# Keys instead of queries masked in a 16-head causal attention, two heads' 64 keys per weight tile, attended values packed for one projection pass (fp32, attention and top-2 mixture of experts on one core)

## The chip, the cores and the metric

One Trainium2 chip, one of its cores. TensorE (PE) does matmuls, PEld is its weight load, VectorE (DVE), ScalarE (ACT) and GpSimd (POOL) do elementwise work, SyncE (SP) issues DMAs; ACT and POOL issue some too. The metric is the device time of one launch in microseconds; lower is better. A profile is one execution, recorded by the hardware.

## What is computed

Sixteen sequences of 256 tokens with 128 features, all in fp32, the weights included:

```python
qkv = (x @ w_qkv).reshape(B, S, 3, 16, 8)
Q, K = apply_rope(Q), apply_rope(K)
attn = softmax(where(causal, Q K^T * 8**-0.5, -1e9))
x1 = layernorm(x + (attn @ V) @ w_proj + b_proj)
logits = x1 @ W_router + b_router
top_vals, top_idx = top_k(logits, 2)            # of 8 experts
w = softmax over the two chosen logits
y = sum over the chosen e of w_e * (relu(x1 @ W1[e] + b1[e]) @ W2[e] + b2[e])
out = layernorm(x1 + y)                         # W1: 128 x 512, W2: 512 x 128
```

## The kernel before

**How the order is set.** The kernel does not issue its instructions where it defines them. `Plan.op` (L441) only records an operation: an engine, a cost (used by the planner that made the order, offline), a function that issues it, what it reads and writes, and for some an alternative on another engine. `emit` (L482) then issues all of them in the order of a literal list, `ORDER` (L339); a second list, `OTHER` (L328), names those that take their alternative engine. Each engine runs its own instructions strictly in that order and waits for others by semaphores. Buffers come from pools that all stages share: k1, k2, k4, k8 in SBUF (1, 2, 4, 8 KB a partition) and, in PSUM, `ps_sc` (one tile of four banks), `ps_o` (one) and `ps_m` (three).

**Attention of one sequence** (`attention(b)`, L830). Transpose x (L837), project q and k (L858), rope on DVE (L866 to L871). The 16 heads of 8 features lie in four row groups of 32 partitions, four heads in each. To use a whole row group for one head, `mask_q` makes four copies of q, each with the rows of one head kept (ACT L881 or DVE L891). A score matmul (L953) has 128 keys of one row group as weights (32 x 128) and two or four masked query copies as 512 moving columns; there are three rounds of four matmuls. The first two have keys 0 to 127 against all queries of two of the four heads, the third keys 128 to 255 against the upper 128 queries of all four. Each round fills the one `sc` tile, ACT takes its exp (L986, 128 x 2048) into SBUF, and POOL sets the entries above the diagonal to zero (`affine_select`, L963, over the first 128 queries of each head).

`weigh` (L1003) multiplies with the values: weights are 32 columns that hold one head's eight values and a column of ones, the ones giving the softmax's denominators; 16 matmuls of 256 columns and 16 of 128. The result has two halves `t`. It is copied out (`o_out`, ACT L1020 or DVE L1024), a DMA gathers the 16 denominators' rows (`load_den`), DVE takes reciprocals (L1039), a DMA puts them back (`load_back`), `stream_shuffle` spreads them over the partitions (L1052, 512 elements), a product divides (L1063, 512), and `project_o` multiplies by w_proj in two passes, one for each half (L1074, four matmuls); the bias is a row of that weight. Then residual (L1086), layernorm statistics (L802, L803) and scaling (L1104). The values come from `project_v` (L904, two matmuls that also give x's part of the router's logits) and are put in place by `place_v` (ACT L913 and L917, or DVE L921 and L925).

**Routing.** The sequences are in four chunks of 4, 4, 2 and 6 (`CHUNKS`). For each, `route` (L1188) takes the two largest logits (DVE L1206 to L1228), counts tokens for each expert (PE L1235), works out addresses (L1240 to L1262; an iota on POOL at L1267), and scatters each token's row to its expert's place in a DRAM heap by indirect DMAs on POOL (L1278): 64 in the program.

**Experts.** 48 calls of `block` (L1490) do 128 or 256 rows each: load rows and weights (SP), transpose (L1537, out by L1564 or L1570), first layer (L1576), relu (ACT L1589 or DVE L1598), second layer (L1606), bias (DVE L1615), the routing weight (ACT L1624 or DVE L1633), and an indirect DMA of each 128 rows to the token's place in DRAM (`send`, POOL L1642, 69 in all). They come in two phases; the last holds the chunk of six sequences. `combine` (L1708) reads the rows back, adds them to x1 (PE L1767 for the last phase, DVE L1777 and L1778 for the other), normalizes and stores. While the last rows are fetched, dummy matmuls run (`keep_warm`, L1875 and L1879, `WARM` = 12). `check` (L1886) looks for overflow; a general path that it would start is not run here.

Of the kernel before, what the change touches and what calls it, by code (L numbers as in the profile page):

```python
# [21 lines left out]
P = 128  # L22
HEADS = 16
HD = 8
# [281 lines left out]
RECIPROCAL = [i // (2 * HD) * (2 * HD) + HD + 1 for i in range(32)]  # L306

WARM = 12
# [20 lines left out]
0 1 4 5 15 16 20 21 27 29 31 32 35 36 37 41 49 51 52 54 68 82 83 84 85 87 102 113 119 122 138  # L329
139 152 154 155 171 185 189 191 208 218 260 261 262 264 281 288 295 297 314 330 331 358 395 428  # L330
451 462 472 474 489 498 503 524 540 559 572 591 594 602 604 610 758 774 797 806 826 838 845 854
857 870 889 890 893 918 925 934 941 953 954 979 994 997 1010 1033 1036 1044 1046 1057 1058 1061
1080 1084 1106 1109 1110 1123 1132 1148 1149 1152 1162 1163 1171 1179 1187 1193 1201 1202 1210
1218 1226 1234 1241 1254 1259 1267 1272 1280 1282 1295 1306 1308 1311 1319 1332 1337 1347 1350
1360 1363 1371 1397 1402 1410 1415 1423 1425 1438 1441 1449 1462 1467 1475 1488 1493 1513 1518
1525 1532 1534 1540
# [3 lines left out]
7 2 0 3 1 6 5 44 27 45 4 28 46 77 9 11 47 53 78 36 48 79 51 52 29 49 12 50 114 30 115 54 61 31  # L340
80 116 62 32 147 148 55 63 117 149 118 81 39 119 83 56 86 58 87 57 85 121 59 122 254 217 82 150
33 218 10 64 8 21 60 151 88 84 35 89 65 184 91 16 185 605 120 19 123 92 66 15 17 255 67 94 90 93
95 68 155 97 154 96 219 20 124 22 131 98 220 606 37 69 18 186 13 221 132 125 187 153 99 70 100
126 101 102 193 127 128 133 152 129 156 188 613 223 134 14 23 130 158 159 42 71 192 157 24 135
190 103 104 136 189 105 161 160 357 25 72 26 358 137 162 194 138 73 163 287 164 165 139 106 288
167 168 224 166 195 191 196 256 222 74 257 198 169 199 75 41 258 107 262 170 140 201 225 200 260
202 289 197 359 231 259 171 108 76 172 232 141 203 109 204 173 290 226 110 291 228 227 263 293
233 142 205 111 143 229 112 174 206 113 360 234 207 235 34 294 175 144 176 230 261 264 268 177
269 208 361 145 324 292 296 178 271 427 325 236 146 394 270 179 180 395 607 272 181 237 182 295
183 238 265 364 626 239 266 326 627 240 327 267 328 209 428 301 628 273 241 365 362 274 275 302  # L350
276 303 298 629 331 242 634 299 210 243 497 630 277 278 304 305 211 363 297 330 632 396 300 244
633 307 306 631 332 397 374 641 640 498 375 279 333 636 308 280 368 398 281 212 369 245 499 366
282 309 310 371 399 402 311 246 367 642 334 372 611 247 213 370 637 604 635 214 283 215 248 38
338 284 376 400 312 313 329 339 567 377 373 285 340 335 314 378 500 639 568 315 336 379 638 380
501 316 341 40 337 286 643 216 381 317 318 612 249 504 506 344 342 250 319 251 401 405 320 406
429 343 648 646 408 619 321 253 322 323 345 645 252 647 534 652 346 653 505 382 654 409 535 507
651 411 412 347 656 43 403 650 503 383 407 404 348 655 414 502 430 384 410 511 657 644 349 658
431 512 415 433 350 536 351 413 508 660 649 432 416 659 385 386 509 667 434 435 352 353 417 387
418 514 515 354 663 537 388 444 665 538 355 542 569 389 445 356 570 390 441 391 510 392 517 513
516 464 393 465 678 518 679 543 680 519 541 540 446 442 436 666 520 539 662 438 437 668 661 664  # L360
681 439 571 682 419 684 521 443 574 618 685 420 696 440 544 573 551 421 552 447 669 683 697 686
522 545 698 422 546 572 672 676 575 699 448 449 548 466 671 675 690 549 609 615 581 688 523 621
800 687 467 468 622 582 450 451 553 700 471 578 423 579 547 701 755 850 472 554 469 610 832 550
883 771 702 473 576 866 867 674 584 689 424 425 931 1014 880 608 990 470 914 977 426 555 524 673
556 784 963 585 670 452 691 453 964 557 804 772 525 475 577 454 476 882 852 677 474 694 770 693
526 896 786 692 695 614 848 849 527 580 455 881 583 946 801 456 478 865 703 1026 528 457 785 620
586 477 479 558 481 559 625 458 753 1002 756 459 529 587 560 835 884 961 588 482 853 851 589 590
854 787 855 561 483 885 591 754 856 886 805 858 806 820 788 1029 484 592 916 480 485 486 487 802
932 460 857 752 488 789 888 461 790 704 859 489 1003 890 593 860 803 490 757 887 758 976 868 889
562 594 759 761 792 794 791 1015 808 900 491 595 596 462 928 793 810 769 492 891 1027 861 493  # L370
863 962 463 494 833 563 892 495 893 597 760 960 564 598 836 929 762 599 894 773 768 1012 1013
915 496 565 864 763 566 795 816 530 531 600 764 601 774 602 862 765 532 767 533 1016 807 817 603
1000 987 796 766 999 775 776 809 811 777 1017 705 778 706 707 812 709 779 1018 710 895 974 965
708 713 780 1019 813 815 781 966 1040 869 711 1041 1025 712 1020 1001 623 837 1038 783 838 870
967 1004 1005 739 748 814 968 819 723 871 989 743 991 840 992 714 898 873 986 821 842 1021 872
749 975 948 750 822 1022 1116 720 834 1030 1031 874 944 719 718 839 725 1006 978 841 843 724
1007 1433 945 1238 721 969 716 973 844 979 993 994 912 1510 715 747 717 1237 970 1028 722 1023
1024 933 934 824 1008 826 875 1404 913 782 726 980 1009 734 897 1250 1508 727 981 818 1090 1329
936 728 732 938 823 735 917 899 971 876 731 1051 982 1460 988 825 983 935 901 736 984 745 1507
937 730 737 1103 918 995 1509 1277 1407 919 1485 996 738 949 902 1354 733 1355 921 1032 1142  # L380
1317 950 930 729 1033 920 1064 922 939 923 845 940 903 997 924 624 1356 740 1482 972 904 925 744
1484 827 1251 1302 1408 1042 927 926 797 1313 947 847 1129 1555 906 746 1326 741 742 905 952 954
951 828 953 1034 907 1065 1066 1091 1380 1035 1434 1239 955 1420 1067 1077 1469 1092 1010 1069
985 1235 1052 1472 846 1011 956 1036 998 908 1117 1068 877 1071 1093 1417 1094 1070 1443 1078
957 959 1053 617 1054 1072 1073 1096 1055 1057 1095 1118 1104 1391 1056 1119 1143 1097 1079 879
1120 1037 1058 1039 1074 941 1395 1080 1382 1330 1121 1122 829 798 1098 878 1263 1432 1130 1274
1105 1303 1106 1099 1082 1076 1100 1144 1059 1381 1123 1084 1043 1081 1145 909 1419 1131 1044
751 1060 1369 958 1262 1107 1083 1045 831 1132 1109 1046 1147 1108 799 1124 1252 1343 1261 1102
1275 1287 1110 1101 942 1146 1248 1125 911 1075 1406 1126 1394 1353 1149 830 1047 910 1288 1133
1048 1265 1379 1279 1421 1049 1148 1134 1304 1378 1280 1352 1291 1135 943 1278 1357 1249 1061  # L390
1111 1358 1292 1314 1293 1150 1367 1136 1266 1393 1267 1085 1112 1050 1368 1458 1137 1301 1151
1359 1062 1063 1365 1113 1152 1290 1305 1128 1115 1138 1473 1127 1139 1289 1268 1264 1456 1114
1236 1339 1086 1430 1294 1360 1306 1300 1269 1140 1295 1276 1431 1253 1254 1281 1328 1327 1087
1383 1361 1270 1362 1282 1384 1271 1141 1445 1255 1283 1240 1272 1154 1256 1241 1307 1284 1318
1319 1257 1435 1285 1242 1470 1258 1436 1089 1259 1316 1153 1437 1308 1315 1243 1331 1438 1385
1244 1088 1418 1363 1219 1187 1486 1245 1447 1211 1260 1386 1246 1320 1332 1309 1195 1474 1321
1220 1247 1475 1296 1221 1422 1273 1310 1471 1366 1163 1387 1203 1364 1297 1188 1388 1476 1322
1423 1196 1222 1439 1298 1179 1311 1477 1392 1189 1340 1323 1171 1197 1424 1389 1342 1483 1324
1312 1396 1198 1397 1478 1370 1444 1390 1440 1299 1223 1398 1204 1371 1341 1479 1425 1399 1344
1205 1345 1333 1164 1190 1155 1426 1487 1427 1441 1334 1372 1212 1335 1325 1428 1286 1191 1480  # L400
1400 1488 1373 1336 1172 1401 1224 1192 1405 1409 1489 1337 1459 1410 1374 1165 1457 1402 1225
1448 1429 1490 1449 1213 1411 1193 1481 1375 1491 1492 1346 1412 1493 1206 1226 1199 1446 1347
1450 1376 1214 1451 1442 1413 1338 1461 1215 1414 1348 1415 1200 1227 1207 1349 1403 1173 1350
# [85 lines left out]
def main_path(  # L489
# [244 lines left out]
    def turn_w():  # L734
        for t in range(2):
            nc.tensor.transpose(ps_w.get()[:, t, :], wproj_sb[:, t, 0:D], ident)
# [1271 lines left out]
```

## Time and profile before

| | |
|---|---|
| Time, three runs | median 429.5 us (427.94 to 432.92) |
| Profiled execution | 430.44 us; its span, first to last instruction, 428.4 |
| Exp L986 | 48 of 1.88 us |
| Causal mask L963 on POOL | 48, 67.3 us |
| Scores L953 / weigh L1003 on PE | 60.6 / 56.7 us |
| Scatter L1278 / send L1642 on POOL | 64 of 0.99 / 69 of 0.99 us |
| Indirect DMA's spacing in a row | 1.28 us (0.97 and 0.30 of issue) |
| Last second layer ends, span ends | 405.5, 428.4 us |

Busy time is the time in which an engine works. In a group's row stand the line, the engine, the tiles and shapes, the number of records, then busy time and the mean of one, then idle time before them and what ended it. One fp32 matmul leaves two records (so "x8" of L953 is a round of four). `<-remote` is a release that the profile can't assign, `issue` is time in which the engine waited for nothing that it shows.

### The profile page before, as it was taken

How to read it: one execution, taken by the hardware profiler on the slowest of the kernel's cores; microseconds unless marked ns; L12 is line 12 of the kernel's file. 1: busy time of each engine (PE TensorE's matmuls, PEld its weight loads, DVE VectorE, ACT ScalarE, POOL GpSimd, SP SyncE). 2: the span in 40 equal slices, each digit the busy share in tenths (PEclk: the TensorE clock that was granted, in tenths of full speed). 3: DMA queues.
4: the chain of work that ended last, by engine and by line, in shares of the span. 5: the costliest groups of instructions: out<-in, count | busy, mean ns of one | idle time of the engine just before them, and what ended most of it. 6: DMA issues, size and time to landing. Idle time of an engine off the chain costs nothing.

```text
span 428.4 us, 8846 instructions
## 1 busy us (share of the span) xinstructions
PE 339.9 (79%) x2811; PEld 242.0 (56%) x2811; DVE 244.3 (57%) x843; ACT 202.6 (47%) x400; POOL 211.3 (49%) x241
## 2 busy tenths in 40 slices
PE   5899999988879786779997539189984896968981
PEld 3444555445434332455896438079873796958870
DVE  2945688995889772644778302015442533575783
ACT  1667778757756653534455211043240322445742
POOL 2346343357786667753025736603467164344432
PEclk9999999998998978969999859669997996997996
DMA  6210020024011015214273445722444443550173
GB/s 190 80 52 8 4 55 3 3 56 68 22 47 29 15 56 159 65 51 115 60 203 114 137 132 141 215 84 87 131 116 123 118 135 100 178 163 29 36 224 107
DMA packets 48436, 39.75 MB, mean 93 GB/s; under 512 B 13807, under 2 KB 38004, under 8 KB 48386
## 3 DMA queue, kind: packets, MB, share of 16 engines
q1 hardware_dynamic: 32658, 26.35, 22.3%
q0 software_dynamic: 4256, 8.47, 5.8%
q10 hardware_dynamic: 11472, 4.31, 4.1%
q8 instruction: 25, 0.41, 0.4%
q14 instruction: 25, 0.20, 0.2%
HBM read 26.90 MB, written 12.01 MB: 91 GB/s over the span
## 4 chain that ended last, share of the span: by engine, by line
PE 46%; issue 13%; DVE 12%; ACT 12%; POOL 7%; another core or an unknown queue 6%; DMA 2%; ACTq 0%; POOLq 0%; DVEq 0%
PE m L1576 13%; PE m L1606 13%; ACT pr L986 9%; PE sc L953 8%; PE ps_o L1003 5%; POOL heap L1278 4%; PE m L1074 3%; POOL pr L963 2%; PE m L858 1%; DVE st L802 1%; PE ps_o L1537 1%; DMA wqk_sb<-in_L_attn_w_qkv_dram 1%; ACT hT L1589 1%; DVE y L1615 1%
## 5 line engine op out<-in xcount | busy, mean ns | idle before, releaser
L1642 POOL DMA_INDIRECT back<-y,rows_in x69 | 68.2, 989 | 104.2 <-ACT y L1624 55.2
L986 ACT ACTIVATE pr<-sc 128x2048 f32<-128x2048 f32 x48 | 90.1, 1878 | 56.3 <-PE sc L953 35.1
L1576 PE MATMUL m<-rT,w 128*128 128x128 f32 (+1 forms) x384 | 77.8, 349 | 33.2 <-DVE y L1615 18.9
L963 POOL TENSOR_SCALAR_AFFINE_SELECT pr<-pr 128x1024 f32<-128x1024 f32 (+1 forms) x48 | 67.3, 1412 | 73.6 <-ACT pr L986 73.5
L1576 PEld LDWEIGHTS m<-rT,w 128*128 128x128 f32 x384 | 61.5, 210 | 41.5 <-DVE y L1615 20.1
L1589 ACT ACTIVATE hT<-m,b_sb 128x128 f32<-128x128 f32 (+1 forms) x124 | 42.2, 417 | 83.9 <-PE m L1576 32.9
L1606 PE MATMUL m<-w_sb,hT 128*128 (+1 forms) x552 | 73.5, 288 | 4.5 <-ACT hT L1589 3.0
L1278 POOL DMA_INDIRECT heap<-x_sb,dest x64 | 63.5, 992 | 22.7 <-issue 20.3
L1606 PEld LDWEIGHTS m<-w_sb,hT 128*128 128x128 f32 x552 | 69.9, 203 | 7.8 <-ACT hT L1589 4.4
L953 PE MATMUL sc<-qTm,qk 32*128 32x512 f32 x384 | 60.6, 673 | 15.1 <-ACT pr L986 12.4
L1003 PE MATMUL ps_o<-pr,va 128*32 128x128 f32 (+1 forms) x1024 | 56.7, 345 | 6.1 <-issue 5.3
L1615 DVE TENSOR_TENSOR y<-m,b_sb 128x128 f32<-128x128 f32 (+1 forms) x48 | 16.7, 348 | 74.9 <-remote 31.5
L1003 PEld LDWEIGHTS ps_o<-pr,va 128*32 128x32 f32 x1024 | 29.6, 113 | 36.9 <-issue 21.8
L953 PEld LDWEIGHTS sc<-qTm,qk 32*128 32x128 f32 x384 | 16.9, 193 | 31.3 <-ACT pr L986 22.7
L1598 DVE TENSOR_SCALAR hT<-m,b_sb 128x128 f32<-128x128 f32 (+1 forms) x68 | 23.3, 399 | 19.7 <-PE m L1576 11.6
L1074 PE MATMUL m<-wproj_sb,o 128*128 128x136 f32 x128 | 20.6, 308 | 4.8 <-issue 3.3
L1074 PEld LDWEIGHTS m<-wproj_sb,o 128*128 128x128 f32 x128 | 18.0, 206 | 11.1 <-issue 5.5
L866 DVE TENSOR_TENSOR part<-m,rope_sb 128x512 f32<-128x512 f32 x16 | 10.9, 680 | 22.5 <-PE m L858 22.4
L858 PE MATMUL m<-xT,wqk_sb 128*128 128x256 f32 x64 | 20.5, 451 | 1.0 <-DMA wqk_sb<-in_L_attn_w_qkv_dram 0.7
L1624 ACT ACTIVATE y<-y,rows_in 128x128 f32<-128x128 f32 x41 | 14.8, 401 | 13.2 <-DVE y L1615 11.5
L881 ACT ACTIVATE qTm<-qk,rows_sb 128x256 f32<-128x256 f32 x40 | 19.5, 506 | 2.1 <-DVE qk L871 2.1
L858 PEld LDWEIGHTS m<-xT,wqk_sb 128*128 128x128 f32 x64 | 12.5, 215 | 11.4 <-issue 5.4
(183 smaller groups left out, 381.5 us busy)
## 6 DMA issues: line engine op xcount, KB each, us to landing
w<-in_L_ffn_W_dram SPq DMA_DIRECT2D x48, 256.0 KB
rows_in<-heap SPq DMA_DIRECT2D x21, 130.0 KB
ys<-back SPq DMA_DIRECT2D x10, 256.0 KB
w_sb<-in_L_ffn_W_dram SPq DMA_DIRECT2D x7, 256.0 KB
rows_in<-heap SPq DMA_DIRECT2D x27, 65.0 KB
ys<-back ACTq DMA_DIRECT2D x6, 256.0 KB
x<-in_L_attn_x_dram ACTq DMA_DIRECT2D x9, 128.0 KB
out_dram<-yout SPq DMA_DIRECT2D x9, 128.0 KB
```

Source lines behind the costliest of these rows:

```text
L858: nc.tensor.matmul(ps_qk.get()[:, s, :], wqk_sb[:, s, :], xT.get(), start=True, stop=True)
L953: nc.tensor.matmul(ps.get()[:, g], qk.get()[rg, 1, ts(kt, P)], qTm.get()[rg, js, kt * P : S], start=True, stop=True,)
L963: nc.gpsimd.affine_select(out=pr.get()[:, :, :, 0:P], in_=pr.get()[:, :, :, 0:P], compare_op=ALU.is_ge, fill=0.0, base=0, pattern=[[0, GRO ...
L986: lambda pr=pr, ps=ps: nc.scalar.activation(pr.get(), ps.get(), AF.Exp),
L1003: nc.tensor.matmul(pso.get()[ts(g, 32), t, kt * P : S], va_t[:, kt, 2 * g + t].rearrange("p u c -> p (u c)")[:, 16 * u : 16 * u + 32], pr. ...
L1074: nc.tensor.matmul(ps_p.get()[:, q, :], o.get()[:, t, ts(q, P)], wproj_sb[:, t, :], start=(t == 0), stop=(t == 1),)
L1278: nc.gpsimd.indirect_dma_start(out=heap[:, :], out_offset=bass.IndirectOffsetOnAxis(ap=dest[:, k, t : t + 1], axis=0), in_=x1_sb[:, t, 0:D ...
L1576: nc.tensor.matmul(ps_h[i].get()[:, c, :], w.get()[:, ts(i * per + c, P)], rT.get()[:, 0 : n * P], start=True, stop=True,)
L1589: nc.scalar.activation(hT.get()[:, at, 0 : n * P], ps_h[i].get()[:, c, :], AF.Relu, bias=bias)
L1598: V.tensor_scalar(hT.get()[:, at, 0 : n * P], ps_h[i].get()[:, c, :], bias, 0.0, ALU.add, ALU.max)
L1606: nc.tensor.matmul(ps_y.get()[:, i, :], hT.get()[:, c, i * P : (i + 1) * P], w2_sb[:, e, c, :].rearrange("p o d -> p (o d)"), start=(c == ...
L1642: put = nc.gpsimd.indirect_dma_start(out=back[:, :], out_offset=bass.IndirectOffsetOnAxis(ap=rows_in.get()[:, i, D : D + 1].bitcast(I32), ...
```

## The change

- **Scores.** The keys are masked instead of the queries. A weight tile holds 64 keys of two heads, one head's 64 columns after the other's (32 x 128), and q itself is the moving side. The tile of 64 keys number c needs only the queries from 64c on. The rounds are: c = 0 (8 matmuls of 256 columns), c = 1 and 3 together (8 of 192, 8 of 64), c = 2 (8 of 128). The exps are of 2048, 2048 and 1024 elements.
- **Causal mask.** Only one 64 x 64 corner of each head is cut: a product with a table of 0 and 1 (`triangle`) over 512, 1024 and 512 elements in place of `affine_select` over 1024, 1024 and 2048. It may run on POOL or DVE; `OTHER` puts 24 of 48 on DVE (15 of 512 and 9 of 1024).
- **Values.** 128 rows hold 64 keys of two heads. `project_v` has eight matmuls with 64 output columns each; `place_v` copies two half-height parts, and the router's part is an operation of its own (`place_r`). Value weights hold both heads in 32 columns, values and ones interleaved; `weigh` has 8 matmuls of 256 columns, then 8 of 192 and 8 of 64, then 8 of 128.
- **Output.** The two halves `t` occupy alternate rows. A new DMA, `pack` (64 KB, one a sequence; 8 on SP's queue, 8 on ACT's), puts the second half's rows between the first half's. Reciprocals go to a tile of their own, shuffle and division take 256 elements instead of 512, and `project_o` is one pass of two matmuls. The bias is added to x beforehand (`x_bias`, 5 on POOL, 11 on DVE).
- **Last blocks.** Of the last phase the last two single blocks (`HOT` = 2) are neither weighed nor sent; POOL sends rows of zeros in their place, early. DVE builds a matrix with the routing weight at each row's token (128 x 1536, compared with token numbers that an iota writes), and PE adds it times the block's result to the sums (`add_here`, 12 times two matmuls of 128 x 128 x 128). `WARM` goes from 12 to 5.
- Pool sizes: k1 19, k2 16, k4 7, k8 5 instead of 18, 18, 5, 6. New literals `ORDER` and `OTHER`. In POOL's new order three masks stand between the scatters of chunks 1 and 2 instead of 15.

```diff
-WARM = 12
+HALF = P // 2
+WARM = 5
+HOT = 2
...
-        qTm = buffer(k4, "qTm", [P, 4, S])
+        kTm = buffer(k4, "kTm", [P, 2, S // HALF, 2, HALF])
...
-                lambda j=j: nc.scalar.activation(
-                    qTm.get()[:, j, :], qk.get()[:, 0], AF.Copy, scale=rows_sb[:, j : j + 1]
-                ),
+            def rows_of_head(j=j):
+                into = kTm.get()[:, j // 2, :, j % 2, :]
+                return into, qk.get()[:, 1].rearrange("p (c k) -> p c k", k=HALF), rows_sb[:, j : j + 1]
+            def mask_k(of=rows_of_head):
+                into, from_, own = of()
+                nc.scalar.activation(into, from_, AF.Copy, scale=own)
...
-            for t in range(NT):
+            for c in range(S // HALF):
+                for u in range(2):
+                    n = VW + E if u == c % 2 else VW
                     nc.tensor.matmul(
-                    ps_v.get()[:, t, :],
-                    xT.get()[:, ts(t, P)],
-                    wvr_sb,
+                        ps_v.get()[u * HALF : (u + 1) * HALF, c // 2, c % 2, 0:n],
+                        xT.get()[:, c * HALF : (c + 1) * HALF],
+                        wv_sb[:, u, 0:n],
...
+        def add_bproj(engine):
+            engine.tensor_tensor(xt.get(), xt.get(), bproj_sb.to_broadcast([P, NT, DR]), ALU.add)
...
+        rounds = [[(0, 0)], [(1, 0), (3, S - HALF)], [(2, 0)]]
+        rounds = [[(t, c, at) for t in range(2) for c, at in r] for r in rounds]
...
-            ps = tile_of(ps_sc, "sc", [P, GROUPS, nj, nq])
-            pr = buffer(k8, "pr", [P, GROUPS, nj, nq])
+            ps = tile_of(ps_sc, "sc", [P, GROUPS, 2, S])
+            pr = buffer(k8 if r < 2 else k4, "pr", [P, GROUPS, 2, nq])
...
-                        ps.get()[:, g],
-                        qk.get()[rg, 1, ts(kt, P)],
-                        qTm.get()[rg, js, kt * P : S],
+                            ps.get()[:, g, t, at : at + S - c * HALF],
+                            kTm.get()[rg, t, c].rearrange("p u k -> p (u k)"),
+                            qk.get()[rg, 0, c * HALF : S],
...
-                nc.gpsimd.affine_select(
-                    out=pr.get()[:, :, :, 0:P],
-                    in_=pr.get()[:, :, :, 0:P],
+                cut = pr.get().rearrange("p g t (b q) -> p (g t) b q", q=HALF)
+                cut = cut[:, :, 0 : 4 : 3] if r == 1 else cut[:, :, 0:1]
+                keep = triangle.rearrange("p (a b q) -> p a b q", a=1, b=1)
+                engine.tensor_tensor(
+                    cut, cut, keep.to_broadcast([P, 2 * GROUPS, 2 if r == 1 else 1, HALF]), ALU.mult
+                )
...
-                            va_t[:, kt, 2 * g + t].rearrange("p u c -> p (u c)")[
-                                :, 16 * u : 16 * u + 32
-                            ],
-                            pr.get()[:, g, 2 * t + u if kt else u, :],
+                            va_t[:, c, 2 * g + t, :],
+                            pr.get()[:, g, t, at : at + S - c * HALF],
...
+            lambda: load(o.get()[1:P:2, 0, :], o.get()[0:P:2, 1, :]),
+            writes=[o],
+            what="pack",
...
-                for t in range(2):
-                    nc.tensor.matmul(
-                        ps_p.get()[:, q, :],
-                        o.get()[:, t, ts(q, P)],
-                        wproj_sb[:, t, :],
+                nc.tensor.matmul(
+                    ps_p.get()[:, q, :], o.get()[:, 0, ts(q, P)], wproj_sb, start=True, stop=True
+                )
...
-                in_=y.get()[:, i, :],
+                in_=nothing if direct else y.get()[:, i, :],
...
+            def place():
+                V.tensor_scalar(
+                    of_row.get(), all_tokens.get(), token.get()[:, 1:2],
+                    rows_in.get()[:, 0, D + 1 : DX], ALU.is_equal, ALU.mult,
+                )
...
+                            put = nc.tensor.matmul(
+                                acc[b].get()[:, i, :], of_row.get()[:, b, i, :], y.get()[:, 0, :],
+                                start=False, stop=False, skip_group_check=True,
+                            )
```

## The prediction, made before the changed kernel was run

> **What bounds the kernel now.** I read the page first (busy shares, chain, groups), then the windows by stage, then the chain of waits inside the attention, then the timeline where the engines go quiet.
>
> ```profile
> PE 339.9 (79%) x2811; PEld 242.0 (56%) x2811; DVE 244.3 (57%) x843; ACT 202.6 (47%) x400; POOL 211.3 (49%) x241
> 6.00:86.00 80.00, 74.05 (x768) 39.48 (x772) 59.62 (x158) 56.01 (x65) 32.64 (x47) 1.00 0.14 39
> 86.00:126.00 40.00, 34.60 (x357) 18.99 (x345) 32.19 (x102) 25.64 (x35) 28.52 (x26) 0.96 0.23 50
> 126.00:154.00 28.00, 23.43 (x215) 11.49 (x213) 23.12 (x72) 16.00 (x24) 19.37 (x18) 0.94 0.09 26
> 154.00:199.40 45.40, 34.16 (x288) 18.25 (x287) 23.46 (x96) 21.93 (x23) 27.03 (x29) 0.81 0.35 98
> 199.40:405.50 206.10, 160.52 (x1150) 144.14 (x1147) 91.37 (x342) 72.34 (x228) 93.55 (x97) 0.88 0.42 120
> 405.50:428.40 22.90, 12.44 (x55) 9.22 (x53) 14.50 (x76) 9.05 (x27) 7.17 (x14) 0.85 0.53 156
> ```
> The rows after the first are stretches: length, then busy time of PE, PEld, DVE, ACT, POOL, then clock and DMA. I cut them at the routing counts of chunks 0, 1 and 2 (PE L1235: 86, 126, 154 us), the first expert block's transpose (199.4) and the last second layer (405.5). Up to 86 us PE is busy for 93% of the time, DVE for 75%. From 86 to 154 DVE is nearest its limit (81%). From 154 on no engine is.
>
> ```profile
> 11.95 1.18 PE sc L953 x8
> 13.12 0.02 issue
> 13.15 1.89 ACT pr L986
> 15.03 0.04 issue
> 15.08 1.19 PE sc L953 x8
> 16.26 0.02 issue
> 16.28 1.89 ACT pr L986
> ```
> The chain (start, length) shows why PE is full and yet waits: one score tile in PSUM, so score (1.18) and exp (1.89) alternate. A round takes 15.08 - 11.95 = 3.13, three a sequence 9.4 us. The other matmuls run under the exps.
>
> ```profile
> 247.43 0.97 POOL L1278 DMA_INDIRECT heap<-x_sb,dest  x1 [0.30 <-issue]
> 248.70 0.97 POOL L1278 DMA_INDIRECT heap<-x_sb,dest  x1 [0.30 <-issue]
> 249.98 0.97 POOL L1278 DMA_INDIRECT heap<-x_sb,dest  x1 [0.30 <-issue]
> 253.05 0.29 DVE L1615 TENSOR_TENSOR y<-m,b_sb 128x128 f32<-128x128 f32 x1 [8.08 <-remote]
> 253.11 0.84 ACT L1589 ACTIVATE hT<-m,b_sb 128x256 f32<-128x256 f32 x2 [10.51 <-remote]
> 253.39 1.22 PE L1576 MATMUL m<-rT,w 128*128 128x256 f32 x2 [7.89 <-DVE y L1615]
> ```
> The last is a stall of everything. POOL issues 12 indirect DMAs in a row (235.9 to 251.0, one per 1.28 us); after about the fifth the other engines start almost nothing until 2 us past the last. The same stands at 157.7-166.5 (7 in a row), 173.1-184.6 (9), 259.2-277.1 (14) and 319.7-332.2 (10). The idle times there add up to about 41 us, some 15 of them in the attention.
>
> **PE.** Scores: before, three rounds of 4 matmuls of 512 columns (L953, 8 records, 1.17). After, 8 x 256, then 8 x 192 + 8 x 64, then 8 x 128. By columns this is 1, 1 and 1/2 of the old round, 2.9 us for 3.5; by weigh's row (L1003: 1.00 for 8 matmuls of 256, 1.01 for 16 of 128) 2.5. Against it: weight loads of 128 columns go from 12 matmuls to 32, 64 records a sequence. L953's 384 loads fill 16.9 us, 0.044 each, because four row groups load together; wholly exposed that is 64 x 0.044 = +2.8. Range 2.5 to 5.8; I take 3.0, near the column count, since loads are already overlapped in that row. Weigh: 3.01 before; after 1.00 + 1.01 + 0.50 = 2.5. Output projection (L1074): 4 matmuls 1.12, after 2, 0.56. Value projection (L904): 2 matmuls 0.73, after 8 short ones with 64 output columns: 0.5 (half the columns in pairs) to 1.06 (L858's row); I take 0.8. Per sequence -0.5 -0.5 -0.56 +0.07 = -1.5, times 16 = -24 us, all in the attention. The new `add_here` is 12 x 2 matmuls of 128 x 128: 0.45 each by half of L1606 (8 records, 0.89), 1.05 by L1767; 7 fewer dummies (L1879, 0.45) give 3.2 back.
>
> The Trainium skill, "TensorE: Matmul & The Clock Gate", section LDWEIGHTS, says that a load's time goes by its columns and not by its rows, so a 32-row load costs what a 128-row one does. That speaks against 64 loads in place of 24. L953's mean load is 193 ns and L1003's, of 32 columns, 113 ns, which agrees. One after another they would be 64 x 0.193 = 12.4 us a sequence and the change far slower; the row's 16.9 us for 384 says they overlap.
>
> **ACT.** Exps: two of 1.88 and one of half the size, 0.94 to 1.0; -0.92 x 16 = -15 us. Six fewer head masks on ACT -3. The value copies become two of 64 partitions (0.37 to 0.74 more each sequence) +6, four more L1020 copies +2, 12 more DMA issues on ACT's queue x 0.4 = +5. About -4. One ring of three rounds: (1.1 + 1.89 + 0.06) + (1.25 + 1.89 + 0.06) + (0.65 + 0.97 + 0.06) = 7.9 us instead of 9.4.
>
> **DVE.** 24 causal masks come over from POOL: 15 of 512 elements at 0.68 to 0.82 (L866 and L1063, both 128x512), 9 of 1024 at 1.25 to 1.6: +21 to +27. Bias into x 11 x 0.44 (L1086, 272 elements) = +5; six more head masks +2.4; place matrices 2 x 1.7 (1,536 elements; L1063's rate gives 2.4, the best rate of a row 1.2) +3; smaller copies +1.5. Off it: shuffle -0.36 (L1052 0.73, half) and division -0.4 (L1063 0.82, half), x 16 = -12; four o_out copies -2.8; others -2. Sum +17 (14 to 22), nearly all before 199 us, where DVE has 138.4 busy of 193.4. It becomes 155.
>
> **POOL.** 48 affine selects (67.3 us) become 24 products: 17 of 512 elements and 7 of 1024. No two-operand product of that size is in the trace on POOL; bounds are DVE's 0.68 for 512 and twice the select's rate, 2.2. I take 1.1 and 2.1: 33 us. Bias sums, iota and tables +6. So -28 us. Under 86 us this hides nothing and costs nothing (POOL is 41% busy).
>
> The Trainium skill, "GPSIMD Engine Reference", section 3.1, gives 2.6 cycles an element at 1.2 GHz for a product of two operands: 1.11 us for 512, no less than the select over 1024 that it replaces (1.12 here). By it the three masks of a sequence stay at 4.4 us against 4.2, and POOL gains only through the 24 that move. No row here shows that product. The sum above stands without it.
>
> Fewer masks leave the scatters closer together. Before, 15 masks break up the scatters of chunks 1 and 2 (runs of 4 to 7 in POOL's queue). After, three are left there: behind the mask of sequence 13, 6 + 8 + 8 = 22 scatters stand with only the short aims (L1267's iotas, 0.15) between them. A burst of n costs about (n - 5) x 1.28. In one piece that is 22 us, where the attention pays 15 now; if `aims12` waits for chunk 2's routing, 14 and 8 cost 12 + 4 = 16. So +1 to +7 between 154 and 199; I take +4.
>
> **New waits.** The `pack` DMA (64 KB) stands beside the denominators' two DMAs and goes in parallel; the division waits for the later. It adds two issues' 0.4 at most, and project_o is queued well behind. The masks on DVE put exp to weigh behind whatever DVE runs; the second score tile does not wait for them.
>
> **The sum, stage by stage.** Up to 86: PE 74.1 - 5.7 = 68.4, DVE 59.6 + 9 = 68, ring 1.5 us a sequence shorter for five sequences: at the old fill (93%) the stage could lose 6, but with two engines at 68 of 80 I take -4. 86 to 154: PE -10, DVE +1; DVE limits: -4. 154 to 199: PE -5, DVE +3.8, four sequences' shorter ring -6, longer bursts +4: these overlap, and I take -3 (-8 to +7). FFN: the same blocks, sends and stalls, three late projections fewer, count 3 some us sooner: -2 (-6 to +4). Tail: fetch still waits for the last ordinary sends (blocks 44 and 45 stay last), two sends fewer to wait for -1, `add_here` 12 x 0.45 to 12 x 1.05 = 5.4 to 12.6 us in the window of 6.2 where dummies ran (405.5 to 411.7): 0 to +6, I take +2. In all -4 -4 -3 -2 +1 = -12. The profiled execution is 428.4 + 2.0 = 430.4, 0.9 above the median of 429.5. So 430.4 - 12 = 418.4; 418.
>
> **Rivals.** (1) Larger gain: the ring's 1.5 us and PE's 24 us come out whole, 430 - 24 - 5 = 401. For it: PE at 93% up to 86 us. Against: DVE's +17. 398 to 408, chance 0.17. (2) DVE takes over: masks wait in its one queue (DVE is 21.56 busy of 24 us between 73 and 97, and there the small L1240, L1260 take 1.0 and 1.7), PE's saving turns into PE idling before weigh: 425 to 434, 0.15. (3) Slower: the burst. The 22 scatters run as one piece (+7), and those of chunk 3 join the sends around them: 20 in a row in the FFN cost (20 - 5) x 1.28 = 19 where the 12 cost 9, +10. With +17 the forecast's -12 is turned into +5, and with the DVE of rival 2 (which takes 6 to 8 of the gain) into +12: 430 + 5 to 430 + 12, 435 to 442. It decides from about 20 in a row. Exposed weight loads come to the same place: at 4.5 us of scores a sequence PE's 16 x 1.5 = 24 is gone. 434 to 450, 0.22. (4) That the last blocks' skipped sends do not shorten the tail, because 44 and 45 still send last, is in the forecast already.
>
> **How the numbers follow.** The forecast, 408 to 425, has 0.46. A difference of 1% (4.3 us) is what a measurement of this kernel tells from none. Faster, below 425.2: 0.46 + 0.17 = 0.63. Same: 0.15. Slower, above 433.8: 0.22. The range reaches from 400 (rival 1 with 0.06 left below) to 438 (half of rival 3 left above): 0.83 inside.
>
> **What would show it.** Right: score records of 1.0 to 1.25, 1.1 to 1.4 and 0.5 to 0.7 and rounds 7.6 to 8 us a sequence; PE near 318 busy, DVE near 262, POOL near 185; count 0 by 82 us, the first block's transpose by 190; the last stretch 22 to 25. Wrong: a score row with loads in it above 1.6; mask rows on DVE above 1 and 1.8; a stall of 20 us or more behind scatters before the first block; an FFN stretch off from 206 by over 6.

## The result: slower on the chip it was timed on, faster on the others

The changed kernel took 444.15 us (median of 4, 442.61 to 446.94), the kernel before, run beside it, 430.75 (427.94 to 432.92): ratio 1.032, interval 1.024 to 1.041. The forecast was 418 with a range to 438: wrong in sign and outside the range. The profiled execution took 443.2, its span is 441.5. Times are medians over the fast runs of a kernel; two of the ten runs of e16 and of e17 were slower and do not count.

One fact has to stand here, since no later number can be read without it. The chips that the runs met are of two kinds. Where the result above and e1 to e4 were run (e1 to e4 on one chip; that of the result is not on record), the kernel before takes 430 us. On four others (e5 to e18) it takes 356 to 360, and there the changed kernel is the faster: 350.09 against 359.65 (e9), ratio 0.974, interval 0.965 to 0.982. A ratio compares with the kernel before on the same chip. Whether it is the chip or its condition at that time is not known.

The page of the changed kernel, and its windows cut at the same events as before: counts 0, 1, 2 at 84.0, 126.9, 162.2, first expert transpose 205.0, end of the last second layer 418. Count 0 starts at 84.9 in the kernel before, a little ahead of the cut at 86. Columns: length, then busy time of PE, PEld, DVE, ACT, POOL, clock, DMA.

```profile
PE 335.2 (76%) x3612; PEld 271.2 (61%) x3612; DVE 255.6 (58%) x892; ACT 199.7 (45%) x433; POOL 192.1 (44%) x231
```

```profile
6.00:84.00 78.00, 67.45 (x1193) 49.11 (x1191) 67.70 (x173) 56.17 (x82) 27.95 (x44) 1.00 0.20 46
84.00:126.90 42.90, 33.07 (x467) 23.65 (x467) 31.08 (x111) 24.97 (x42) 23.32 (x22) 0.79 0.20 53
126.90:162.20 35.30, 27.51 (x328) 19.99 (x328) 21.27 (x82) 19.54 (x34) 16.73 (x19) 0.68 0.15 45
162.20:205.00 42.80, 33.75 (x479) 21.71 (x474) 27.12 (x96) 18.03 (x21) 21.88 (x20) 0.84 0.35 93
205.00:418.00 213.00, 157.47 (x1064) 143.18 (x1063) 92.78 (x353) 71.57 (x230) 89.84 (x95) 0.88 0.40 117
418.00:441.50 23.50, 14.76 (x92) 12.73 (x90) 14.68 (x80) 8.14 (x25) 7.47 (x14) 0.89 0.55 158
```

The first stretch has the busy times of the forecast (PE 67.5 and DVE 67.7 for 68 and 68), but count 0 comes only 1 us sooner (84.0 for 84.9). Count 2 is 8 us later than before, the first block 6, the last second layer 13. The clock column has fallen from 0.96 and 0.94 to 0.79 and 0.68 in the second and third stretch.

Two places show what happens there. First the clock (windows of 8 us in the changed kernel):

```profile
78.00:86.00 8.00, 3.74 (x85) 2.70 (x84) 7.37 (x24) 4.12 (x7) 2.60 (x4) 0.94 0.06 17
86.00:94.00 8.00, 7.94 (x102) 4.81 (x102) 6.61 (x26) 3.90 (x6) 1.55 (x2) 0.64 0.11 25
94.00:102.00 8.00, 4.33 (x76) 3.15 (x78) 4.00 (x14) 4.37 (x9) 6.29 (x6) 1.00 0.39 94
102.00:110.00 8.00, 7.93 (x88) 5.97 (x92) 5.31 (x16) 3.24 (x4) 4.32 (x3) 0.50 0.33 95
```

DVE is nearly full from 78 to 86 (7.37 of 8 us), PE has work for 3.74 of 8, and the stretch behind it runs at 0.64. From 94 to 102 DVE has work for only 4.00 of 8 us, but POOL issues seven indirect DMAs (95.4 to 105.3); PE has work for 4.33, and the stretch behind it runs at 0.50. A score round of 1.15 us takes 2.09 in such a stretch (at 89.7) and one of 1.32 takes 2.41 (at 130.3). One at 101.9 takes 4.71, more than half the clock explains. On a chip without stalls (e9) the first of the two slow stretches is there too (2.09 at 89.5), the second is not. The Trainium skill, "TensorE: Matmul & The Clock Gate", section "HAM oscillation — how this bites in real kernels", says that gaps of the matmul engine beyond some 3.4 us halve its clock. Here the longest idle times of PE ahead of the two slow stretches are 2.94 us (before 84.0) and 3.20 us (before 101.9), so a little less was enough.

Second the stall (timeline of the changed kernel, the row of 17 indirect DMAs from 265.7 to 287.5):

```profile
278.50 0.33 PE L1645 MATMUL m<-ident,rows_in 128*128 128x128 f32 x1 [3.47 <-issue]
...
281.44 0.97 POOL L1385 DMA_INDIRECT heap<-x_sb,dest  x1 [0.30 <-issue]
...
285.27 0.97 POOL L1750 DMA_INDIRECT back<-y,rows_in  x1 [0.30 <-issue]
286.55 0.97 POOL L1750 DMA_INDIRECT back<-y,rows_in  x1 [0.30 <-issue]
290.01 0.42 DVE L1723 TENSOR_TENSOR y<-m,b_sb 128x256 f32<-128x256 f32 x1 [18.87 <-remote]
290.14 0.27 ACT L1678 COPY rT<-m 128x128 f32<-128x128 f32 x1 [11.69 <-remote]
```

DVE and ACT wait for matmuls that the same timeline has ended: ACT's copy for the transpose of 278.50. The trace's semaphore events have PE's counter go up at 277.28 and not again until 289.99. The data of the indirect DMAs are not late: of the 17 of this row, 15 post their last semaphore update 2.1 to 3.8 us after they start, some of them while PE's counter stands still (two updates are not in the trace). So it looks as if the engines had work and lacked the news of it. The ends of matmuls are modelled in the profile, so that the matmuls themselves ended late is not excluded. What holds them back, the trace does not show.

### The profile page after: what moved, and what is told of

The parts are those of the page before. It is cut to its first block, busy times and chain, and to the rows that moved or that the text cites. A ratio compares the mean times of both kernels' runs of the same rounds, so it can differ in the third digit from the quotient of the medians.

```text
span 441.5 us, 10556 instructions
## 1 busy us (share of the span) xinstructions
PE 335.2 (76%) x3612; PEld 271.2 (61%) x3612; DVE 255.6 (58%) x892; ACT 199.7 (45%) x433; POOL 192.1 (44%) x231
## 5 line engine op out<-in xcount | busy, mean ns | idle before, releaser
L1080 ACT ACTIVATE pr<-sc 128x2048 f32<-128x2048 f32 (+1 forms) x48 | 76.5, 1593 | 54.2 <-PE sc L1050 29.3
L1050 PE MATMUL sc<-qk,kTm 32*128 32x192 f32 (+3 forms) x1024 | 65.2, 359 | 27.4 <-ACT pr L1080 21.3
L1050 PEld LDWEIGHTS sc<-qk,kTm 32*128 32x128 f32 x1024 | 48.2, 205 | 43.6 <-ACT pr L1080 30.1
L1063 POOL TENSOR_TENSOR pr<-pr,triangle 128x512 f32<-128x512 f32 (+1 forms) x24 | 38.5, 1615 | 65.8 <-ACT pr L1080 65.7
L1106 PE MATMUL ps_o<-pr,va 128*32 128x256 f32 (+3 forms) x1024 | 51.1, 334 | 3.0 <-issue 2.0
L1106 PEld LDWEIGHTS ps_o<-pr,va 128*32 128x32 f32 x1024 | 29.4, 120 | 20.2 <-issue 10.0
L1063 DVE TENSOR_TENSOR pr<-pr,triangle 128x512 f32<-128x512 f32 (+1 forms) x24 | 21.4, 899 | 25.2 <-ACT pr L1080 25.2
L1706 DVE TENSOR_SCALAR hT<-m,b_sb 128x256 f32<-128x256 f32 (+1 forms) x66 | 23.6, 412 | 11.3 <-PE ps_o L1645 5.2
L1678 ACT COPY rT<-ps_o 128x128 f32<-128x128 f32 (+1 forms) x15 | 4.5, 303 | 36.3 <-PE ps_o L1645 23.2
L921 PE MATMUL m<-xT,wqk_sb 128*128 128x256 f32 x64 | 20.5, 452 | 0.5 <-DVE xT L911 0.5
L947 ACT ACTIVATE kTm<-qk,rows_sb 128x256 f32<-128x256 f32 x34 | 16.5, 504 | 2.2 <-DVE qk L934 2.0
L976 PE MATMUL m<-wv_sb,xT 128*64 128x64 f32 (+1 forms) x256 | 13.3, 249 | 2.5 <-issue 1.3
```

What stands on the lines that cost most here:

```text
L921: nc.tensor.matmul(ps_qk.get()[:, s, :], wqk_sb[:, s, :], xT.get(), start=True, stop=True)
L947: nc.scalar.activation(into, from_, AF.Copy, scale=own)
L1050: nc.tensor.matmul(ps.get()[:, g, t, at : at + S - c * HALF], kTm.get()[rg, t, c].rearrange("p u k -> p (u k)"), qk.get()[rg, 0, c * HALF ...
L1063: engine.tensor_tensor(cut, cut, keep.to_broadcast([P, 2 * GROUPS, 2 if r == 1 else 1, HALF]), ALU.mult)
L1080: lambda pr=pr, ps=ps, nq=nq: nc.scalar.activation(pr.get(), ps.get()[:, :, :, 0:nq], AF.Exp),
L1106: nc.tensor.matmul(pso.get()[ts(g, 32), t, c * HALF : S], va_t[:, c, 2 * g + t, :], pr.get()[:, g, t, at : at + S - c * HALF], start=(c == ...
```

## The experiments

**e1, all products on POOL** (`OTHER` without the 24 entries of the causal products):

```diff
-OTHER: 24 of 48 `mask` operations on DVE
+OTHER: none
```

> The changed kernel with all 48 causal products on POOL (none on DVE); nothing else moved. Theory A (DVE took PE's place as the bound before the first block, PE starves behind it and its granted clock halves: 0.79 and 0.69 between 84 and 153 us): DVE loses 21.4 us of work before 205 us, the first block's transpose comes earlier by 5 to 15 us, the clock there rises above 0.85, and the time falls from 444 to 430-440. Rival B (what costs is the products' latency on POOL, 1.30 and 2.37 us each): POOL gets 31 us more before 205, weigh waits for it, and the time rises to 446-460. Rival C (rows of indirect DMAs on POOL): the products break the rows again, as in the kernel before; idle time of all three engines in the rows before the first block goes away (3 us), the part after count 3 stays at 188 us.

443.94 us, ratio 1.036 (1.029 to 1.043): no change from the changed kernel's 444.15. Count 0 came 6 us later (90.1), count 2 5 us earlier (157.3), the first layer at 207.5 for 207.1. The rows of scatters ahead of the first block are 5, 4, 5, 4, 8 and 7 long in place of 7, 5, 4, 6 and 15. A's gain did not come, and neither did B's loss; e12 shows what they hide.

**e2, PE filled** (both projections issued twice into the same place):

```diff
-            for s in range(2):
+            for s in (0, 1, 0, 1):
...
-            for q in range(NT):
+            for q in (0, 1, 0, 1):
```

> The changed kernel with the matmuls of project (q, k) and of project_o issued twice each, the second time into the same place: 1.6 us more PE work a sequence, 26 us in all, about what the change took away. Theory A (PE idles and its clock is halved, so that work saved on PE is not time saved): the time moves by less than a quarter of the added work, 438-450, and the mean granted clock from 6 to 205 us rises. Rival (PE is still the bound and the change failed because its own matmuls got longer): +15 to +26 us, 459-470.

455.20 us, ratio 1.058 (1.052 to 1.064), between both theories. The two doubled groups grew by 21 us, not 26 (project 20.5 to 34.0, project_o 11.0 to 19.0), and cost 11: a microsecond of PE work is worth 0.5.

**e3 and e4, spaced indirect DMAs**, in the changed kernel and in the kernel before:

```diff
+    pause = const.tile([P, 448], F32, name="pause")
...
         def scatter(t, k):
...
+            nc.gpsimd.memset(pause, 0.0)
...
         def send(i):
...
+            nc.gpsimd.memset(pause, 0.0)
```

> The changed kernel with a memset of 448 elements on POOL (about 0.45 us) behind every indirect DMA, so that a row has one about every 1.75 us instead of 1.28. Theory C1 (the stall of every engine comes from indirect DMAs issued faster than their queue takes them): the stalls of 7 us and more (240, 279, 328 us) go, 20 to 25 us of idle time, and the time falls to 420-435. Rival C2 (the stall comes with their number, whatever their spacing): the rows and stalls get longer by a third, 450-465. Rival C3 (the stalls cost nothing, other waits take their place): 440-450.

> The kernel before with the same memset of 448 elements behind every indirect DMA. C1: the 31 us in which PE, DVE and ACT all stand still fall to under 10, and the time from 430 to 405-422. C2: stalls longer, 435-450. C3: 427-435.

e3: 389.22 us, ratio 0.907 (0.900 to 0.913). e4: 393.83 us, ratio 0.917 (0.911 to 0.923). With 133 memsets of 0.51 us more on POOL, the changed kernel loses 55 us and the kernel before 36. That is the sign of C1, and more than its ranges of 420-435 and 405-422; its reason, a queue that falls behind, is not shown. In e3, 52 indirect DMAs stand in one row with a period of 1.63 us, and the engines work beside it (window of that row; below it the changed kernel's row of 17 and the 2 us behind it):

```profile
239.60:323.60 84.00, 68.74 (x480) 63.22 (x478) 33.64 (x100) 22.08 (x70) 75.61 (x104) 0.96 0.48 135
```

```profile
265.70:290.00 24.30, 8.79 (x63) 7.35 (x62) 1.00 (x3) 4.09 (x12) 16.93 (x19) 0.78 0.41 119
```

PE is busy for 82% of the first and 36% of the second. The order of the two kernels has turned round: with the pauses the changed one is 4.6 us ahead.

**e5, e11, e14 and e18, one element instead of 448, in the changed kernel; e10 and e15 in the kernel before** (`nc.gpsimd.memset(pause[:, 0:1], 0.0)`):

> The changed kernel with a memset of one element a partition (about 0.1 us) behind every indirect DMA, in place of the 448 of the run before. If the stall hangs on the spacing of the indirect DMAs, a row's period goes from 1.28 only to about 1.35 and most of the stalls stay: 425-444. If it hangs on nothing else running on POOL between two of them, any instruction ends it: 383-395, and rather below 389 since POOL does less.

> The kernel before with a memset of one element a partition (about 0.1 us) behind every indirect DMA. On a chip with stalls: 390-400 of 430 if any instruction of POOL between two indirect DMAs ends the stall, 415-430 if their spacing does. On a chip without: 357-362.

> The changed kernel with the same one-element memset. On a chip with stalls: 380-392 if any instruction ends the stall, 425-444 if the spacing does. On a chip without: 349-352, that is the changed kernel's own time or up to 3 us more.

> The changed kernel with a one-element memset behind every indirect DMA. On a chip with stalls: 380-392 if any instruction of POOL between two of them ends the stall, 425-444 if their spacing does. On a chip without: 349-352, a repeat.

> The kernel before with the same memset. On a chip with stalls: 390-400 if any instruction ends the stall, 415-430 if the spacing does. On a chip without: 357-360, a repeat.

> The changed kernel with a one-element memset behind every indirect DMA. On a chip with stalls: 380-392 if any instruction of POOL between two of them ends the stall, 425-444 if the spacing does. On a chip without: 347-352, a repeat.

All six met chips without stalls and tell nothing of the question: 349.61, 349.61, 349.45 and 349.31 us for the changed kernel (ratios 0.978, 0.976, 0.976, 0.980, each within 0.969 to 0.987), 357.05 and 356.93 for the kernel before (0.994, interval 0.990 to 0.999, and 0.998, 0.993 to 1.003). On such a chip the small memset costs nothing, so these runs are used as references of their kernels there.

**e6 and e7, spaced only behind the scatters of the first three chunks** (`if b + n < B:` ahead of the memset in `scatter`, none in `send`). These are 40 and not the 52 that the expectations name: the traces have 40 memsets of 0.50 us.

> The changed kernel with the memset of 448 elements only behind the scatters of the first three chunks (52 of 133 indirect DMAs). The whole pause brought 55 us; by the stages of that run 14 us of it were gained by count 2, 19 by the first layer, the rest after it. If the stages are independent this one gives 444 - 17 to 21 = 423-427; if the earlier start only runs into the same stalls of the expert part, 435-444.

> The same for the kernel before: 52 scatters of the first three chunks spaced. The whole pause brought 36 us, 6 of them by the first layer: 422-426 if the stages are independent. Against the run before it tells how much of the change's extra 18 us of stall lies before the first expert block: 10 to 15 by the stages, under 5 if only the rows after count 3 matter.

e6: 359.97 us, ratio 1.010 (1.006 to 1.013); e7: 369.88, ratio 1.035 (1.027 to 1.044), on a chip where the kernel before takes 357. As a division of the stalls they failed: there were none. They show the price of the pauses, 10 and 13 us (359.97 against e5's 349.61, 369.88 against 357). They also compare the kernels: the changed one is 9.9 us ahead.

Beside e3 and e4 they show more. Up to the first expert block the code of e6 is that of e3, and that of e7 is that of e4, on the two kinds of chip. The times of counts 0, 1, 2 and of the first layer:

| | count 0 | count 1 | count 2 | first layer |
|---|---|---|---|---|
| e3 (chip with stalls) / e6 (without) | 83.8 / 83.7 | 123.1 / 122.5 | 147.7 / 147.0 | 188.2 / 187.2 |
| e4 (chip with stalls) / e7 (without) | 85.3 / 85.0 | 123.3 / 123.3 | 152.8 / 152.8 | 194.6 / 195.2 |
| changed kernel / e9, no pauses | 84.0 / 83.8 | 126.9 / 119.0 | 162.2 / 141.9 | 207.1 / 179.0 |
| kernel before / e10 | 84.9 / 84.9 | 125.8 / 121.1 | 154.0 / 145.0 | 200.7 / 181.7 |

With the pauses the two kinds of chip agree within 1.0 us; without them they differ by 28 and 19 us. So ahead of the first block the difference of the two kinds hangs on indirect DMAs that follow each other without a pause; no other difference shows there.

**e8, spaced and PE filled**:

> The changed kernel with the 448-element pauses, and with project and project_o issued twice (26 us more PE work, as in the run with filled PE, which cost 11 us without the pauses). If PE is the bound of the attention once the stalls are gone: 389 + 18 to 26 = 407-415. If PE waits for DVE and ACT there: 389-397.

395.65 us, ratio 1.108 (1.100 to 1.115), on a chip without stalls; its reference, e3, ran on the other, so its own question stays open. Its expert part tells something else: from the first layer to the end of the last second layer it takes 172.3 us, and e3, on the chip with stalls, 169.2. With pauses in the experts too, nothing of the stall shows there, though e8 has a few doubled matmuls in that part (without pauses the changed kernel takes 211.0 and e9 148.0).

**e9, the changed kernel itself again:**

> The changed kernel itself, beside the kernel before on the same chip. The runs with the pause behind the first scatters met a chip on which the kernel before takes 357 us and shows no stall in 64 indirect DMAs in a row; the first four runs and the result met one with 430 and stalls. If the stalls decide the sign: on a chip with stalls 1.02 to 1.04 of the kernel before; on one without, 0.97 to 0.99 (about 348-352 where the kernel before takes 357). If the change is slower by itself: above 1 on both.

350.09 us, 0.974 (0.965 to 0.982): the sign turns (its interval reaches across the 2% at which a difference is counted as clear, but not to 1). Windows of e9, cut at its counts (84, 119, 142), first block (179) and last second layer (326.8); the seventh line is the longest row of indirect DMAs, 64 with no pause:

```profile
6.00:84.00 78.00, 67.70 (x1195) 49.51 (x1193) 67.79 (x174) 56.22 (x83) 28.04 (x44) 1.00 0.20 47
84.00:119.00 35.00, 28.07 (x467) 19.87 (x466) 30.77 (x110) 26.18 (x46) 22.65 (x22) 0.86 0.24 66
119.00:142.00 23.00, 21.11 (x330) 15.92 (x330) 21.39 (x78) 17.20 (x31) 16.06 (x15) 0.84 0.23 64
142.00:179.00 37.00, 27.46 (x496) 19.26 (x497) 30.21 (x107) 18.98 (x24) 24.05 (x24) 0.91 0.43 118
179.00:326.80 147.80, 139.53 (x1037) 129.33 (x1038) 91.10 (x346) 70.22 (x229) 89.70 (x95) 1.00 0.58 166
326.80:350.60 23.80, 14.87 (x93) 12.85 (x91) 14.70 (x80) 7.93 (x25) 8.23 (x15) 0.88 0.54 160
206.00:288.00 82.00, 80.70 (x598) 75.76 (x598) 39.95 (x127) 28.13 (x84) 62.72 (x66) 1.00 0.64 180
```

The same for the kernel before on that chip (e10):

```profile
6.00:85.00 79.00, 72.79 (x751) 38.59 (x751) 58.66 (x153) 54.98 (x64) 32.69 (x47) 1.00 0.15 39
85.00:121.10 36.10, 32.13 (x360) 17.79 (x361) 31.05 (x102) 26.57 (x36) 27.31 (x37) 1.00 0.26 53
121.10:145.00 23.90, 19.53 (x216) 10.23 (x214) 22.09 (x78) 17.06 (x25) 22.10 (x29) 1.00 0.11 32
145.00:181.70 36.70, 29.23 (x320) 15.84 (x320) 26.47 (x98) 22.11 (x24) 30.66 (x49) 0.95 0.41 120
181.70:332.90 151.20, 144.62 (x1110) 133.38 (x1111) 89.40 (x338) 69.91 (x225) 103.09 (x186) 0.99 0.57 165
332.90:356.40 23.50, 12.86 (x57) 9.49 (x55) 14.83 (x79) 9.88 (x29) 8.00 (x18) 0.84 0.53 153
```

Beside 64 indirect DMAs PE is busy for 98%: neither their number nor their spacing stops anything on this chip. On the other three, e6, e13 and e16 show the same (64, 70 and 70 in a row, PE busy for 80.8 of 82, 89.3 of 91 and 89.1 of 91 us). Stretch by stretch the changed kernel is 1.0, 1.1 and 0.9 us ahead, 0.3 behind, 3.4 ahead in the experts, 0.3 behind in the tail. From 84 to 142 us DVE is busy for 90% of the time, and PE's clock is 0.86 and 0.84 where the kernel before has 1.00.

**e12 and e13, e1 and e2 on a chip without stalls:**

> The changed kernel with all 48 causal products on POOL, which moved nothing on the chip with stalls (443.9 against 444). On a chip without stalls, where the changed kernel takes 350.1: if DVE bounds the attention there (68 of 78 us busy up to count 0, 21 us of it products), 342-348; if the products' 1.30 and 2.41 us on POOL are the longer wait for weigh, 352-360.

> The changed kernel with project and project_o issued twice, 26 us more PE work in the attention. It cost 11 us on the chip with stalls. On a chip without: if PE still bounds, 350 + 20 to 26 = 370-376; if PE, DVE and ACT share the bound, 355-364; if PE's saving is worth nothing there, 350-353.

e12: 377.38 us, ratio 1.052 (1.045 to 1.059), 28 us more than e14 on the same chip. What DVE gives up does not show as time, because weigh now waits for POOL's products (waits of e12: total, times, longest):

```profile
PEld ps_o L1106 <- POOL pr L1063: 19.5, 8, 5.9
...
PE ps_o L1106 <- POOL pr L1063: 17.5, 7, 5.7
```

The first layer of e12 starts at 205.4 us, that of e1 at 207.5: with all products on POOL the chip with stalls costs 2 us ahead of the first block, for the changed kernel 28. Either the products break the rows, or the stalls pass while weigh waits for POOL anyway; these runs do not tell which. e13: 361.12 us, ratio 1.011 (1.007 to 1.015), 11.7 more than e14 for 21 us of matmuls (project 34.7 us for 20.7 in e9, project_o 17.8 for 10.6): 0.55 us for each, as in e2. PE shares the bound here too.

**e16 and e17, all products, and only the seven long ones, moved to DVE** (entries added to `OTHER`):

> The changed kernel with all 48 causal products on DVE (0.69 and 1.25 us each, against 1.30 and 2.41 on POOL). All on POOL cost 27 us on a chip without stalls. If POOL's slow products are what weigh waits for and DVE has room, 340-348 where the changed kernel takes 350 (on a chip with stalls also less POOL work among the scatters, so longer rows: 440-450 of 444). If DVE is by now as full as PE, its 20 us more make it 352-362.

> Only the seven 1024-element products that the change left on POOL (2.41 us each) moved to DVE (1.25): +8.8 us of DVE work, -16.9 of POOL. Latency of POOL's products as the limit: 345-349 for 350; DVE as the limit: 352-358; balanced: within 2 of 350.

e16: 356.6 us, ratio 1.000 (0.996 to 1.004); e17: 353.7, 0.995 (0.991 to 0.999); 7.3 and 4.4 us more than e18 on that chip. DVE has little room: 8.8 us of DVE work more in e17 cost half of it. Of the four splits tried the changed kernel's half and half is the fastest where there are no stalls. Its order was made for that split, and no run here makes a new order for another.

## Why the prediction was wrong

**The step that failed: added stall was put at nothing in two terms of the sum, "86 to 154: ... DVE limits: -4" and "FFN: the same blocks, sends and stalls", -2.** The stalls were seen in the profile of before, and rival 3 named what they could do, with a chance of 0.22. The table cuts all runs at the same events: count 0, count 2, the first layer, the end of the last second layer. A kernel's stall is its profile where the result was timed, less its profile on a chip without stalls (e10 and e9).

| us | forecast | measured | stall before | stall changed | change without stalls |
|---|---|---|---|---|---|
| to count 0 | -4 | -0.9 | 0.0 | 0.2 | -1.1 |
| to count 2 | -4 | +9.2 | 9.0 | 20.2 | -2.0 |
| to the first layer | -3 | -1.9 | 10.1 | 7.7 | +0.4 |
| to the last second layer | -2 | +6.2 | 53.3 | 63.0 | -3.5 |
| tail | +1 | +0.5 | -0.3 | -0.2 | +0.4 |
| all | -12 | +13.1 | 72.0 | 90.9 | -5.8 |

So the change adds 19 us of stall: 11 between counts 0 and 2 and 10 in the experts, where the sum had none, and it takes 2 away between count 2 and the first layer, where the sum had put "longer bursts +4". (By medians, 430.75 and 444.15 against 359.65 and 350.09, the stalls cost 71 and 94.) The 22 scatters of that burst ran as 6, 1 and 15. That the sum of rival 3, 435 to 450, has the measured time in it is in part luck: its +10 in the experts came, its one long row ahead of them did not.

That the stalls hang on unpaused indirect DMAs, and that without them the sign turns, is shown (e3 with e6, e4 with e7, e3 with e8, e9). Why the changed kernel's are larger is not. In the experts its longest row has 17 for 14, which fits; between counts 0 and 2 its rows are 7, 1, 5, 1, 4 and 6 long for 4, 2, 2, 6, 1, 1, 3 and 5, worth 3 us more by the (n - 5) x 1.28 of the prediction and not 11. There PE's clock is 0.79 and 0.68 for 0.96 and 0.94, and PE is busy for 60.6 us, in e9 for 49.2 (kernel before 58.0, e10 51.7). By these, some 5 of the 11 us are the slower clock behind the stalls; this is an estimate, and the rest stays open. Idle time read at 41 us was little over half of the 72, since it counted only the stretches in which engines stand still.

**What would have been right without stalls.** e9 is 9.6 us below the kernel before (7.0 below e10), for a forecast of -12 that has the +4 for bursts in it. Up to the first block the gain is less than forecast (-2.7 for -11), in the experts more (-3.5 for -2).

**PE's 24 us.** PE's busy time up to the first block fell by 9 us only (144 against 154, the four windows above added). The rounds at full clock are 1.15, 1.32 and 0.73, 3.20 in all for 3.0: 3 us. The rest is chiefly the clock: 28.07 x 0.14 + 21.11 x 0.16 + 27.46 x 0.09 = 10 us of e9's busy time up to 179 is lost to it by this estimate, under 2 in e10. The sum took PE's records at full clock although it made PE wait more; that row stood in the profile of before (0.81 between 154 and 199).

**DVE and POOL.** The products took 0.69 and 1.25 us on DVE (forecast 0.68 to 0.82, 1.25 to 1.6) and 1.30 and 2.37 on POOL (1.1 and 2.1). The Trainium skill's "GPSIMD Engine Reference", section 3.1, gave 1.11 for 512 elements by its cycles per element; the first row below is 17% above it.

```profile
L1063 POOL TENSOR_TENSOR pr<-pr,triangle 128x512 f32<-128x512 f32 x17 | 22.1, 1302 | 54.3 <-ACT pr L1080 54.3
...
L1063 POOL TENSOR_TENSOR pr<-pr,triangle 128x1024 f32<-128x1024 f32 x7 | 16.6, 2374 | 11.4 <-ACT pr L1080 11.4
...
L1063 DVE TENSOR_TENSOR pr<-pr,triangle 128x1024 f32<-128x1024 f32 x9 | 11.3, 1252 | 4.6 <-ACT pr L1080 4.6
...
L1063 DVE TENSOR_TENSOR pr<-pr,triangle 128x512 f32<-128x512 f32 x15 | 10.3, 688 | 20.6 <-ACT pr L1080 20.6
```

DVE's sum was right up to count 0 (67.7 for 68); up to the first block DVE grew by 12 us (150.2 in e9, 138.3 in e10) for +17. That DVE is nearest its limit from 86 to 154 was misread: by the prediction's own rows PE is busy for 85% there and DVE for 81. Without stalls DVE is ahead (89% for 86 in e10, 90 for 85 in e9), and the gain there was 2 us for a forecast of 4. Rival 2 has the effect right without stalls, that PE's gain is lost in the attention, but its cause, weigh waiting for products on DVE, is not in e9: weigh's longest wait there is 4.4 us, once, for a copy of values, and PE waits most for exps (17.8 us, in e10 11.1).

**Right.** The weight loads do not come out: 64 of 128 columns a sequence lie beside matmuls of four row groups (3.20 us of scores, not 5.8). The tail is the same (23.4 us for 22.9), and the skipped sends bring nothing that shows.

**Open.** What holds the other engines back while POOL issues indirect DMAs; why the change makes the stalls 19 us longer; whether the spacing or any instruction between them helps (the one-element runs never met a stall); whether the chip or its condition at the time decides.

## What to carry to other kernels

A stall that stands still in a profile must be priced as a term of its own, in every stretch that has its trigger and not only where it stands out; here the stalls cost the changed kernel 19 us more than the kernel before, twice what the change gains without them. Work taken from a full engine is worth its price only while its neighbours stay below it: with PE and DVE both near 87% (68 of 78 us), a microsecond of PE was worth 0.5, and by the estimate above PE, made to wait, lost a third of the forecast saving to its clock (8 of 24 us). Time such a change on more than one chip before believing the sign.

## What the runs showed of the hardware

- Where the result was timed, DVE, ACT and PE stand still for up to 11 us at a time beside rows of back-to-back indirect DMAs (1.28 us each). On four other chips they do not (PE 80.7 of 82 us busy beside 64 of them). The kernel before takes 430 us on the one kind and 356 to 360 on the other.
- On the chip with the stall a memset of 0.51 us behind each indirect DMA brought 36 and 55 us, and made the two kinds of chip equal within 1.0 us ahead of the first block; without the stall, 40 such memsets cost 10 and 13.
- The granted clock was 0.50 behind 8 us in which PE was busy for 4.33, with 3.20 us of idle time in one piece; a score round of 1.32 us then takes 2.41.
